# Reordering one graph-network kernel in four places: ScalarE's steps between copies in layer 0, the tail into layer 1, a short tile's list transfers, and the negative sums of layer 2

## The chip, the cores and the metric

The kernel runs on one core of a Trainium2 chip. The metric is the device time of one execution in microseconds (us). Of the kernel before, three runs gave 1071.43 us in the median (1069.46 to 1074.38). Engines are named as in the profile: PE is TensorE (PEld its weight loads), DVE is VectorE, ACT is ScalarE, POOL is GpSimd and SP is SyncE, which here only issues transfers. Every engine works through its own instructions in the order in which the program gave them, and waits on semaphores for what others produce.

## The reference

Four graph layers on 2708 nodes with 128 features, each behind a LayerNorm and a ReLU. `adj` is a dense float32 matrix of 2708 x 2708 (29 MB) with about 0.6% of it, and the diagonal, not zero.

```python
# --- layer 0 ---
h = jnp.maximum(_layernorm(x, axis=-1), 0.0)
x = x + (adj.T @ h) * (1 / adj.sum(axis=0))[:, None]          # 1/0 taken as 0
# --- layer 1 ---
h = jnp.maximum(_layernorm(x, axis=-1), 0.0)
s, d = h @ msg_w[:, :D].T, h @ msg_w[:, D:].T
messages = jax.nn.gelu(s[:, None, :] + d[None, :, :] + msg_b, approximate=False)
aggregated = jnp.einsum('ijd,ij->id', messages, adj)
new = concatenate([h, aggregated], -1) @ upd_w.T + upd_b
x = x + layernorm(gelu(new) + h) * ln_w + ln_b
# --- layer 2 ---
h = jnp.maximum(_layernorm(x, axis=-1), 0.0)
msg = jax.nn.relu((adj @ h) @ W_msg.T + b_msg)
x = x + _gru_cell(msg, h, W_ih, W_hh, b_ih, b_hh)
# --- layer 3: two attention heads, mask = (adj > 0) or the diagonal ---
```

## The kernel before, in words

The nodes are cut into 22 tiles of 128 rows (`NT`; the last has 20, `TAIL`), and these into six groups: five of four tiles, the last of two. Columns are also counted in blocks of 124 (`JB`, 22 of them), because layer 1 works on lists: for every row and block the eight largest entries and their places.

**Layer 0** (0 to about 224 us) reads `adj` once. The loop over `order` goes through five column cuts c (some 512 wide) and for each through six row groups s; a sixth, narrow cut c = `LAST` = 5 (tiles named `z`) is worked beside c = 4. For each (c, s): VectorE lists the rows (`list_cut`, MAX8 and FIND_INDEX8, lines 346 and 348); GpSimd copies the blocks near the diagonal without the diagonal (`mask_near`); `work_cut` has PE transpose the tile (line 387), ScalarE copy the transpose to SBUF (`aT`, line 391), ScalarE's queue write it to `adjT` in memory (line 354, one copy behind), and PE add `adj.T @ h` up in PSUM (`products`, line 373, with a column of ones for the column sums). Cut tiles come from a ring of four buffers, loaded by SP's queue three steps ahead. ScalarE also does LayerNorm steps: `sum_rows` (line 249), `sum_squares` (line 256), whose small steps go to GpSimd, and `normal_rows` (line 136); in c = 0 for the rows of `x`, in a block after each `work_cut`, later for the finished group c - 1, whose new rows are made by `spread` (line 430). `turn_rows`, `destinations` and `split_destinations` prepare `d` of layer 1 for a group. Group 4 and 5 are entered on VectorE by `enter` (reciprocal at line 417, sum into `xs` at 439, statistics) and `rows`. The narrow cut's piece s - 1 is worked after (4, s), its last piece after the loop, and its lists (`list_last`) are taken between layer 1's first steps.

**Layer 1** (to about 600 us) takes one tile per `period(t)`. Before the first, a list of steps written out by hand (`for step, n in (...)`, lines 985 to 996) fills the pipe. In a period, `pass_on` has PE transpose the rows' places (`p_w`, line 740), ScalarE copy them, and SP send them to memory (`passed`, line 744) and back to all partitions (`spread`, line 746); `columns` compares them on VectorE (line 754), which PE's `p_m` products need (lines 805 and 809). `finish_rows` wants `later` (lines 661 and 662, also SP). Tile 21 (20 rows) is listed with other geometry: `load_wide` in period 14, `list_wide` at the end of period 15 (`WIDE_AT`), MAX8 and FIND_INDEX8 on up to 120 partitions (lines 634 and 636) and then twelve small transfers on SP's queue (line 639) that bring the results to `val` and `col`.

**Layer 2** (603 to 785 us) reads `adjT` in six chunks of 512 columns, in five pieces each (`aggregate`; three buffers `a2`): load by SP's queue, three or four ScalarE sums of the negative parts per piece ("looks", line 1241, which end up in `below` and a flag), masks on VectorE and GpSimd, and up to five products into `p_agg` (line 1254). Between products `spend` and `advance` let steps of the chunk before run (`finish_chunk`): `aggc` (line 1265), `hc` (copy at line 151), `p_m` and `msg` (1275, 1277), the gates (1290), `nn` (1298), `h` and `z` (line 136), `z3T` (1331), `hv` (1341 to 1343). Layer 3 follows until 1070 us.

Of the kernel before, what the change touches and what calls it, by code (L numbers as in the profile page):

```python
# [60 lines left out]
def listed_layers(ctx: ExitStack, tc: tile.TileContext, x, adj, w, out, flag):  # L61
# [184 lines left out]
    def sum_rows(t, k):  # L246
        for q in range(t, t + k):
            junk = pool.tile([P, D], F32, name="junk")
            nc.scalar.activation(junk, xs[:, q, :], AF.Copy, accum_out=flat[:, 0, q : q + 1])
        v = flat[:, 0, t : t + k]  # L250
        nc.gpsimd.tensor_scalar(v, v, -1.0 / D, None, ALU.mult)

    def sum_squares(t, k):
# [5 lines left out]
        shift, ve, rstd, tmp = (flat[:, q, t : t + k] for q in range(4))  # L259
        nc.gpsimd.tensor_scalar(ve, ve, 1.0 / D, EPS, ALU.mult, ALU.add)  # L260
        nc.gpsimd.tensor_tensor(rstd, ve, minus_half[:, 0:k], ALU.pow)
        nc.gpsimd.tensor_tensor(tmp, rstd, rstd, ALU.mult)
        nc.gpsimd.tensor_tensor(tmp, tmp, ve, ALU.mult)
        nc.gpsimd.tensor_scalar(tmp, tmp, -0.5, 1.5, ALU.mult, ALU.add)
        nc.gpsimd.tensor_tensor(rstd, rstd, tmp, ALU.mult)
        nc.gpsimd.tensor_tensor(shift, shift, rstd, ALU.mult)

    def normal_rows(dst, t, k):
        scale_rows(
            [dst[:, q, 0:D] for q in range(t, t + k)], tiles_of(xs, t, k),  # L270
            flat[:, 2, t : t + k], flat[:, 0, t : t + k], AF.Relu,
        )
# [83 lines left out]
    def work_cut(c, s):  # L356
# [24 lines left out]
        for js in turns:  # L381
# [13 lines left out]
            ))  # L395
            if c > 0 and todo and gk == 4:
                products(todo.pop(0))
        for n in todo:
# [26 lines left out]
    def spread(g):  # L425
# [5 lines left out]
        nc.gpsimd.tensor_tensor(xs[:, t : t + k, :], xs[:, t : t + k, :], part_x[:, 0:k, :], ALU.add)  # L431
# [28 lines left out]

    order = [(c, s) for c in range(LAST) for s in range(len(GROUPS))]
    mask_near(0, 0)
    for i, (c, s) in enumerate(order):
        g0, gk = GROUPS[s]
        list_cut(c, s, g0)
        if i == 0:
            scale_rows(
                [h0[:, q, 0:D] for q in range(4)], tiles_of(xs, 0, 4), *factors(*state.pop(("m", -1))), AF.Relu
            )
        for n in range(g0 + 1, g0 + gk):  # L470
            list_cut(c, s, n)
        off = 1 if c < LAST - 1 else 0
        if c > 0 and s == off:
# [7 lines left out]
        if i == 0:  # L481
            sum_rows(*GROUPS[1])
        work_cut(c, s)

        if c == 0:
            for stage, g in (
# [1385 lines left out]
```

## Time and profile before

| | |
|---|---|
| median of three runs | 1071.43 us (1069.46 to 1074.38) |
| the profiled execution | 1072.07 us, span 1070.3 us |
| PE, PEld, DVE | 932.0 us (87%), 815.0 (76%), 791.3 (74%) |
| ACT, POOL | 531.7 us (50%), 473.3 (44%) |
| granted TensorE clock, mean | 0.943 of full speed |
| copies of transposes, line 391 | 122, 67.0 us busy, 75.5 us idle before them |
| products of layer 0, line 373 | 880, 121.5 us |
| products of layer 2, line 1254 | 264, 111.2 us, 19.2 us idle before them (13.2 for transfers) |

A row of instructions gives the start and the busy time in us, the engine and the line, the operation, what it writes and reads, the shape and the number; in brackets stands the idle time of the engine just before it and what ended it. Since engines wait in their own order, an idle engine counts only where others wait for it in turn. Shares of the whole span mix layers: in layer 0 from 60 to 190 us the DMA engines are full, in layers 2 and 3 PE is.

### The profile page before, as it was taken

The page shows a single profiled execution, that of the slowest core. Times are in us where ns is not written, and L with a number is a line of the kernel's source. Part 1 is how long each engine was busy: PE and PEld are TensorE (multiplying, and loading weights), DVE is VectorE, ACT ScalarE, POOL GpSimd, SP SyncE. Part 2 cuts the span into 40 slices and gives each one's busy share as a digit, 9 for nine tenths or more (in the row PEclk, how much of TensorE's full clock was granted, in tenths as well). Part 3 has the DMA queues.
Part 4 walks back from the last instruction along what each step waited for, and adds up shares of the span by engine and source line. Part 5 has one row for each costly group of instructions (what it writes and reads, how often), then busy time and mean ns, then how long its engine had stood idle before and what let it go on. Part 6 is the DMA issues. An engine that isn't in the chain of part 4 may idle for free. (4 is left out here: it accounts for less than half of the span.)

```text
span 1070.3 us, 23391 instructions
## 1 busy us (share of the span) xinstructions
PE 932.0 (87%) x8632; PEld 815.0 (76%) x8632; DVE 791.3 (74%) x2740; ACT 531.7 (50%) x1511; POOL 473.3 (44%) x596
## 2 busy tenths in 40 slices
PE   4899898952999999999699759899979999989983
PEld 3799787842899999999699624344468899989982
DVE  7899899468677788979474445555578977997793
ACT  5645554533666667666476366777732200330142
POOL 6222231322987778997576352334310300250042
PEclk9899899975899999999899879999989999999996
DMA  8799899412333333332221435565410000000000
GB/s 287 236 318 373 280 367 365 153 54 81 118 116 104 118 106 121 102 108 91 82 83 56 148 111 172 183 203 203 124 38 20 8 8 1 2 15 6 2 15 16
DMA packets 77091, 133.65 MB, mean 125 GB/s; under 512 B 13980, under 2 KB 29456, under 8 KB 76966
## 3 DMA queue, kind: packets, MB, share of 16 engines
q1 hardware_dynamic: 56986, 99.92, 28.4%
q10 hardware_dynamic: 19980, 32.14, 8.3%
q8 instruction: 70, 1.15, 0.4%
q14 instruction: 55, 0.45, 0.1%
HBM read 85.41 MB, written 30.87 MB: 109 GB/s over the span
## 5 line engine op out<-in xcount | busy, mean ns | idle before, releaser
L723 POOL TENSOR_SCALAR put<-count,line,value 128x128 f32<-128x128 f32 x176 | 202.1, 1161 | 40.3 <-DVE value L712 27.1
L1106 PE MATMUL att<-hv,wt 128*128 128x129 f32 x1672 | 195.5, 278 | 8.8 <-DVE wt L1076 7.3
L1106 PEld LDWEIGHTS att<-hv,wt 128*128 128x128 f32 x1672 | 191.8, 194 | 11.9 <-DVE wt L1076 7.2
L809 PE MATMUL p_m<-d,cols 124*128 124x128 bf16 (+1 forms) x1452 | 164.3, 222 | 7.5 <-DVE cols L754 7.5
L805 PE MATMUL p_m<-s,sel 128*128 128x128 bf16 x1452 | 163.7, 222 | 6.1 <-ACT g L817 6.0
L1076 DVE SCALAR_TENSOR_TENSOR wt<-row,lift,mask 128x1024 f32<-128x1024 f32 (+1 forms) x132 | 138.1, 1075 | 24.5 <-PE att L1106 24.4
L120 POOL TENSOR_TENSOR n_r<-n_r,minus_half 128x4 f32<-128x4 f32 (+1 forms) x27 | 38.9, 1440 | 241.3 <-DVE n_r L119 237.5
L1254 PE MATMUL p_agg<-a,hs 128*128 128x512 f32 (+2 forms) x264 | 111.2, 563 | 19.2 <-DMA a<-adjT 13.2
L830 PE MATMUL agg<-put,g 128*128 128x128 f32 (+1 forms) x968 | 122.9, 279 | 0.0
L373 PE MATMUL sums<-h,a 128*128 128x129 f32 (+1 forms) x880 | 121.5, 287 | 0.0
L830 PEld LDWEIGHTS agg<-put,g 128*128 128x128 f32 x968 | 113.6, 192 | 0.0
L373 PEld LDWEIGHTS sums<-h,a 128*128 128x128 f32 (+1 forms) x880 | 112.6, 202 | 0.9 <-issue 0.2
L805 PEld LDWEIGHTS <-sel 128*128 128x128 bf16 x1452 | 105.1, 99 | 7.8 <-issue 7.3
L809 PEld LDWEIGHTS <-cols 124*128 124x128 bf16 (+1 forms) x1452 | 104.4, 99 | 7.9 <-DVE cols L754 7.9
L391 ACT COPY aT<-p_T 128x512 f32<-128x512 f32 (+2 forms) x122 | 67.0, 564 | 75.5 <-PE p_T L387 47.6
L732 ACT ACTIVATE put<-mine,value 128x128 f32<-128x128 bf16 x308 | 100.5, 391 | 0.0
L817 ACT ACTIVATE g<-p_m 128x512 f32<-128x512 f32 x132 | 72.7, 551 | 55.8 <-PE agg L830 43.1
L1254 PEld LDWEIGHTS p_agg<-a,hs 128*128 128x128 f32 (+1 forms) x264 | 48.3, 196 | 67.8 <-issue 52.0
L387 PE MATMUL p_T<-ident,a 128*128 128x128 f32 (+1 forms) x440 | 72.6, 286 | 30.4 <-ACT aT L391 23.9
L348 DVE FIND_INDEX8 col<-val,a 128x8 uint16<-128x124 f32 x342 | 91.5, 278 | 0.0
L346 DVE MAX8 val<-a 128x8 f32<-128x124 f32 x342 | 78.7, 270 | 12.1 <-DMA a<-in_adj 12.1
L387 PEld LDWEIGHTS p_T<-ident,a 128*128 128x128 f32 (+1 forms) x440 | 53.4, 146 | 39.3 <-ACT aT L391 27.5
(269 smaller groups left out, 1571.8 us busy)
## 6 DMA issues: line engine op xcount, KB each, us to landing
adjT<-aT ACTq DMA_DIRECT2D x105, 256.0 KB
a<-adjT SPq DMA_DIRECT2D x20, 1280.0 KB
spread<-passed SPq DMA_DIRECT2D x22, 704.0 KB
later<-sel SPq DMA_DIRECT2D x22, 616.0 KB
a<-in_adj SPq DMA_DIRECT2D x5, 1152.0 KB
a<-in_adj SPq DMA_DIRECT2D x5, 1120.0 KB
a<-in_adj SPq DMA_DIRECT2D x5, 1088.0 KB
a<-in_adj SPq DMA_DIRECT2D x5, 1056.0 KB
```

The source lines that it names most:

```text
L346: nc.vector.max(val[0:m, n, b, :], v)
L348: nc.vector.max_index(col[0:m, n, b, :], val[0:m, n, b, :], v)
L373: nc.tensor.matmul(accs[c][q // 2][0:k, q % 2, :], a[0:m, n - g0, e : e + k], h0[0:m, n, :], start=(n == 0 and q % 2 == 0), stop=(n == NT ...
L387: nc.tensor.transpose(p[0:k, i * iw + q * P : i * iw + q * P + m], a[0:m, q, e : e + k], ident[0:m, 0:m])
L723: nc.gpsimd.tensor_scalar(st["put", 0][:, b, :], count, st["line"][:, b : b + 1], st["value"][:, b : b + 1], ALU.is_equal, ALU.mult,)
L732: nc.scalar.activation(st["put", 1][:, b - HP, :], st["mine"][:, b - HP, :], AF.Identity, scale=st["value"][:, b : b + 1])
L805: nc.tensor.matmul(p[:, b - b0, :], st["sel"][:, b, :], s3[:, q, t % 2, :], start=(q == 0), stop=False)
L809: nc.tensor.matmul(p[:, b - b0, :], st["cols"][0:kb, b, :], d3[0:kb, b, q, :], start=False, stop=(q == 2))
L830: nc.tensor.matmul(agg, g[:, b - 4 * k, :], put, start=(b == 0), stop=False)
L1076: nc.vector.scalar_tensor_tensor(wt[:, 0:n], row[:, k, c : c + n], lift[:, j, k : k + 1], mask[:, j, c : c + n], op0=ALU.max, op1=ALU.mult,)
L1106: nc.tensor.matmul(banks[s // 3][:, s % 3, :], wt[:, q * P : (q + 1) * P], hv[:, j, k, :], start=(v < 2 and s // 3 not in touched), stop=( ...
L1254: nc.tensor.matmul(pa[:, 0:n], h[0:k, j, :], a[0:k, j - j0, 0:n], start=(j == 0), stop=(j == NT - 1))
```

## The change

Four groups of edits, none of which alters the arithmetic that PE does.

In layer 0 `sum_rows`, `sum_squares`, `normal_rows` and `spread` become generators, and `work_cut` takes one step of them (two in cut 0) after each copy of a transpose, and the rest behind the last. The normal rows of group 0 no longer precede the copies of the first step, they are steps among them; the statistics of group 1 are taken by VectorE's `moments` and `factors`. The narrow cut's pieces are worked after (4,1) to (4,4) by a table `PARTS`, all before (4,5), with `mask_near` for each ahead; `turn_rows(3)` stands before (4,5).

After the loop, the narrow cut's sums are copied at once, group 5 is entered before group 4, and the written-out list of layer 1's first steps is rearranged to fit.

`list_wide` no longer issues its twelve transfers; `place_wide` does so in period 16, at k = 3, behind `columns`.

In layer 2 the looks of a piece stand behind products 2 and 4 of the piece (or at its end) instead of behind its load.

```diff
--- before.py
+++ after.py
@@ -243,33 +243,40 @@
             nc.scalar.copy(dst[1], r)
             nc.gpsimd.tensor_tensor(dst[2], r, dst[1], ALU.subtract)
 
-    def sum_rows(t, k):
+    def sum_rows(g):
+        t, k = GROUPS[g]
         for q in range(t, t + k):
             junk = pool.tile([P, D], F32, name="junk")
             nc.scalar.activation(junk, xs[:, q, :], AF.Copy, accum_out=flat[:, 0, q : q + 1])
-        v = flat[:, 0, t : t + k]
-        nc.gpsimd.tensor_scalar(v, v, -1.0 / D, None, ALU.mult)
-
-    def sum_squares(t, k):
+            if q == t + k - 1:
+                v = flat[:, 0, t : t + k]
+                nc.gpsimd.tensor_scalar(v, v, -1.0 / D, None, ALU.mult)
+            yield
+
+    def sum_squares(g):
+        t, k = GROUPS[g]
         for q in range(t, t + k):
             junk = pool.tile([P, D], F32, name="junk")
             nc.scalar.activation(
                 junk, xs[:, q, :], AF.Square, bias=flat[:, 0, q : q + 1], accum_out=flat[:, 1, q : q + 1]
             )
-        shift, ve, rstd, tmp = (flat[:, q, t : t + k] for q in range(4))
-        nc.gpsimd.tensor_scalar(ve, ve, 1.0 / D, EPS, ALU.mult, ALU.add)
...
-        nc.gpsimd.tensor_tensor(shift, shift, rstd, ALU.mult)
-
-    def normal_rows(dst, t, k):
-        scale_rows(
-            [dst[:, q, 0:D] for q in range(t, t + k)], tiles_of(xs, t, k),
-            flat[:, 2, t : t + k], flat[:, 0, t : t + k], AF.Relu,
-        )
+            if q == t + k - 1:
+                shift, ve, rstd, tmp = (flat[:, r, t : t + k] for r in range(4))
+                nc.gpsimd.tensor_scalar(ve, ve, 1.0 / D, EPS, ALU.mult, ALU.add)
...
+                nc.gpsimd.tensor_tensor(shift, shift, rstd, ALU.mult)
+            yield
+
+    def normal_rows(dst, g, rstd=None, shift=None):
+        t, k = GROUPS[g]
+        for q in range(k):
+            r, b = (flat[:, 2, t : t + k], flat[:, 0, t : t + k]) if rstd is None else (rstd, shift)
+            scale_rows([dst[:, t + q, 0:D]], [xs[:, t + q, :]], r[:, q : q + 1], b[:, q : q + 1], AF.Relu)
+            yield
 
     RING = 4
     WINDOW = CH + 16 * (len(GROUPS) - 2)
@@ -353,7 +360,9 @@
         if written:
             nc.scalar.dma_start(*written.pop())
 
-    def work_cut(c, s):
+    def work_cut(c, s, between=()):
+
+        steps = iter(between)
 
         g0, gk = GROUPS[s]
         t0, tk = GROUPS[c]
@@ -393,8 +402,12 @@
             written.append((
                 adjT[0:k, js[0] : js[0] + n, i0 : i0 + iw], aT[0:k, 0 : n * iw].rearrange("p (j i) -> p j i", j=n)
             ))
+            for _ in range(2 if c == 0 else 1):
+                next(steps, None)
             if c > 0 and todo and gk == 4:
                 products(todo.pop(0))
+        for _ in steps:
+            pass
         for n in todo:
             products(n)
 
@@ -428,7 +441,9 @@
         part_x = pool.tile([P, 4, D], F32, bufs=1, name="part_x")
         for q in range(k):
             nc.scalar.activation(part_x[:, q, :], sums_of(g, q), AF.Identity, scale=inv[:, t + q : t + q + 1])
-        nc.gpsimd.tensor_tensor(xs[:, t : t + k, :], xs[:, t : t + k, :], part_x[:, 0:k, :], ALU.add)
+            if q == k - 1:
+                nc.gpsimd.tensor_tensor(xs[:, t : t + k, :], xs[:, t : t + k, :], part_x[:, 0:k, :], ALU.add)
+            yield
 
     def enter(g):
 
@@ -458,19 +473,53 @@
     for q in range(2):
         nc.gpsimd.memset(wheres[q], 0.0)
 
+    def in_turn(*steps):
+        for step in steps:
+            yield from step
+
+    def first_steps(s):
+
+        if s == 0:
+            return in_turn(
+                sum_rows(2), normal_rows(h0, 0, *state.pop(("f", 0))), normal_rows(h0, 1, *state.pop(("f", 1)))
+            )
+        return in_turn(*(
+            step for ok, step in (
+                (s < LAST, sum_squares(s + 1)), (s < LAST - 1, sum_rows(s + 2)), (s < LAST, normal_rows(h0, s + 1))
+            ) if ok
+        ))
+
+    def next_steps(c, s):
+
+        off = 1 if c < LAST - 1 else 0
+        stage = s - 1 - off
+        if stage == 0:
+            return spread(c - 1)
+        if stage == 1:
+            return sum_rows(c - 1)
+        if stage == 2:
+            return sum_squares(c - 1)
+        if stage == 3:
+            return normal_rows(h, c - 1)
+        return ()
+
+    PARTS = {1: (0,), 2: (1, 2), 3: (3,), 4: (4, 5)}
     order = [(c, s) for c in range(LAST) for s in range(len(GROUPS))]
     mask_near(0, 0)
     for i, (c, s) in enumerate(order):
         g0, gk = GROUPS[s]
         list_cut(c, s, g0)
         if i == 0:
-            scale_rows(
-                [h0[:, q, 0:D] for q in range(4)], tiles_of(xs, 0, 4), *factors(*state.pop(("m", -1))), AF.Relu
-            )
-        for n in range(g0 + 1, g0 + gk):
-            list_cut(c, s, n)
-        off = 1 if c < LAST - 1 else 0
-        if c > 0 and s == off:
+            state["f", 0] = factors(*state.pop(("m", -1)))
+            list_cut(c, s, g0 + 1)
+            state["m", 1] = moments(tiles_of(xs, *GROUPS[1]), "n0")
+            list_cut(c, s, g0 + 2)
+            state["f", 1] = factors(*state.pop(("m", 1)))
+            list_cut(c, s, g0 + 3)
+        else:
+            for n in range(g0 + 1, g0 + gk):
+                list_cut(c, s, n)
+        if c > 0 and s == (1 if c < LAST - 1 else 0):
             invert(c - 1)
         if i + 1 < len(order):
             mask_near(*order[i + 1])
@@ -478,36 +527,19 @@
             load_cut(*order[i - 1 + RING])
         if c == LAST - 2:
             load_cut(LAST, s)
-        if i == 0:
-            sum_rows(*GROUPS[1])
-        work_cut(c, s)
-
-        if c == 0:
-            for stage, g in (
-                ((sum_rows, 2), (sum_squares, 1), (sum_rows, 3), (sum_squares, 2), (normal_rows, 1)),
-                ((sum_rows, 4), (sum_squares, 3), (normal_rows, 2)),
-                ((sum_rows, 5), (sum_squares, 4), (normal_rows, 3)),
-                ((sum_squares, 5), (normal_rows, 4)),
-                ((normal_rows, 5),),
-                (),
-            )[s]:
-                stage(h0, *GROUPS[g]) if stage is normal_rows else stage(*GROUPS[g])
-        elif s == 1 + off:
-            spread(c - 1)
-        elif s == 2 + off:
-            sum_rows(*GROUPS[c - 1])
-        elif s == 3 + off:
-            sum_squares(*GROUPS[c - 1])
-        elif s == 4 + off:
-            normal_rows(h, *GROUPS[c - 1])
+        if (c, s) == (LAST - 1, LAST):
+            turn_rows(LAST - 2)
+        work_cut(c, s, first_steps(s) if c == 0 else next_steps(c, s))
         if c > 1 and s == 0:
             turn_rows(c - 2)
         if c > 1 and s == 1:
             destinations(c - 2)
         if c > 1 and s == 3:
             split_destinations(c - 2)
-        if c == LAST - 1 and s > 0:
-            work_cut(LAST, s - 1)
+        if c == LAST - 1:
+            for z in PARTS.get(s, ()):
+                mask_near(LAST, z)
+                work_cut(LAST, z)
 
         if (c, s) == (0, 3):
             nc.sync.dma_start(msg_wT, w["msg_wT"])
@@ -523,20 +555,19 @@
             nc.gpsimd.tensor_copy(src_self[:, 0, :], msg_wT[:, 0, :])
             nc.gpsimd.tensor_tensor(src_self[:, 1, :], msg_wT[:, 0, :], msg_wT[:, 1, :], ALU.add)
 
-    def list_last(n):
-        list_cut(LAST, n // 4, n)
-
-    for n in range(4):
-        list_last(n)
-    enter(LAST - 1)
-    turn_rows(LAST - 2)
-    destinations(LAST - 2)
-    work_cut(LAST, LAST)
     write_one()
     for q, k in ((0, P), (1, TAIL)):
         nc.scalar.copy(last_sums[0:k, q, :], accs[LAST][0][0:k, q, :])
-    for s in range(len(GROUPS)):
-        mask_near(LAST, s)
+
+    def list_last(n):
+        list_cut(LAST, n // 4, n)
+
+    list_last(0)
+    enter(LAST)
+    for n in range(1, 4):
+        list_last(n)
+    enter(LAST - 1)
+    destinations(LAST - 2)
     l0.close()
 
     gate_b = late.tile([P, 2], F32, name="gate_b")
@@ -634,6 +665,10 @@
                 nc.vector.max(tops[0:m, q, :], cols[0:m, q, :])
             for q, m in enumerate(rows_of):
                 nc.vector.max_index(tops_at[0:m, q, :], tops[0:m, q, :], cols[0:m, q, :])
+            state["tops"] = tops, tops_at
+
+        def place_wide():
+            tops, tops_at = state.pop("tops")
             for i, (b, k) in enumerate(pieces):
                 for dst, src in ((val, tops), (col, tops_at)):
                     nc.sync.dma_start(
@@ -952,6 +987,8 @@
                     put_more(t + 1, k)
                 if k == 3 and c:
                     columns(t + 1)
+                if k == 3 and t == WIDE_AT + 1:
+                    place_wide()
                 if k == 3 and b:
                     place(t + 2)
                 if k == 4 and a:
@@ -984,12 +1021,12 @@
 
         puts = ExitStack()
         for step, n in (
-            (count_rows, 0), (rank, 0), (list_last, 4), (select_rows, 0), (describe, 0), (rows, 4),
-            (list_last, 5), (list_last, 6), (count_next, 0), (turn_rows, 4), (split_destinations, 3),
-            (finish_rows, 0), (fetch_both, 0), (rank, 1), (destinations, 4), (enter, 5), (place, 0), (pass_on, 0),
-            (sources, 0), (select_rows, 1), (split_destinations, 4), (rows, 5), (describe, 1),
-            *((list_last, n) for n in range(7, 12)), (columns, 0), (turn_rows, 5), (destinations, 5),
-            (finish_rows, 1), (fetch_both, 1), (rank, 2), (split_destinations, 5), (place, 1), (select_rows, 2),
+            (count_rows, 0), (rank, 0), (rows, 5), (list_last, 4), (select_rows, 0), (describe, 0), (rows, 4),
+            (turn_rows, 5), (split_destinations, 3), (list_last, 5), (list_last, 6), (count_next, 0), (turn_rows, 4),
+            (finish_rows, 0), (destinations, 4), (fetch_both, 0), (rank, 1), (destinations, 5),
+            (split_destinations, 4), (place, 0), (pass_on, 0), (split_destinations, 5), (sources, 0),
+            (select_rows, 1), (describe, 1), *((list_last, n) for n in range(7, 12)), (columns, 0),
+            (finish_rows, 1), (fetch_both, 1), (rank, 2), (place, 1), (select_rows, 2),
             *((list_last, n) for n in range(12, 17)), (describe, 2), *((list_last, n) for n in range(17, NT)),
             (close_lists, 0),
         ):
@@ -1233,15 +1270,6 @@
             nc.sync.dma_start(a[:, 0:whole, 0:n], adjT[:, j0 : j0 + whole, c : c + n])
             if whole < jn:
                 nc.sync.dma_start(a[0:TAIL, whole, 0:n], adjT[0:TAIL, NT - 1, c : c + n])
-            for m, q0, q1 in ((P, 0, min(2, whole)), (P, 2, min(4, whole)), (P, 4, whole), (TAIL, whole, jn)):
-                if q1 > q0:
-                    junk = pool.tile([P, 2, CH], U8, name="junk2")
-                    i = len(looked)
-                    looked.append(i)
-                    nc.scalar.activation(
-                        junk[0:m, 0 : q1 - q0, 0:n], a[0:m, q0:q1, 0:n], AF.Relu, scale=-1.0,
-                        accum_out=below[0:m, i : i + 1],
-                    )
@@ -1256,6 +1284,18 @@
                 )
                 spend(n / CH)
                 advance()
+                look = {2: ((P, 0, min(2, whole)),), 4: ((P, 2, min(4, whole)),)}.get(j - j0, ())
+                if j == j0 + jn - 1:
+                    look = ((P, 0, whole), (TAIL, whole, jn)) if jn < PIECE else (*look, (P, 4, whole))
+                for m, q0, q1 in look:
+                    if q1 > q0:
+                        junk = pool.tile([P, 2, CH], U8, name="junk2")
+                        i = len(looked)
+                        looked.append(i)
+                        nc.scalar.activation(
+                            junk[0:m, 0 : q1 - q0, 0:n], a[0:m, q0:q1, 0:n], AF.Relu, scale=-1.0,
+                            accum_out=below[0:m, i : i + 1],
+                        )
 
         def finish_chunk(t0, k0, pa):
```

More of the change, by code (lines that the diff above doesn't have):

```diff
@@ L258, in sum_squares @@
             )
-        shift, ve, rstd, tmp = (flat[:, q, t : t + k] for q in range(4))
-        nc.gpsimd.tensor_scalar(ve, ve, 1.0 / D, EPS, ALU.mult, ALU.add)
[L261 to L265, printed above, removed]
-        nc.gpsimd.tensor_tensor(shift, shift, rstd, ALU.mult)
-    def normal_rows(dst, t, k):
-        scale_rows(
-            [dst[:, q, 0:D] for q in range(t, t + k)], tiles_of(xs, t, k),
-            flat[:, 2, t : t + k], flat[:, 0, t : t + k], AF.Relu,
-        )
+            if q == t + k - 1:
+                shift, ve, rstd, tmp = (flat[:, r, t : t + k] for r in range(4))
+                nc.gpsimd.tensor_scalar(ve, ve, 1.0 / D, EPS, ALU.mult, ALU.add)
+                nc.gpsimd.tensor_tensor(rstd, ve, minus_half[:, 0:k], ALU.pow)
+                nc.gpsimd.tensor_tensor(tmp, rstd, rstd, ALU.mult)
+                nc.gpsimd.tensor_tensor(tmp, tmp, ve, ALU.mult)
+                nc.gpsimd.tensor_scalar(tmp, tmp, -0.5, 1.5, ALU.mult, ALU.add)
+                nc.gpsimd.tensor_tensor(rstd, rstd, tmp, ALU.mult)
+                nc.gpsimd.tensor_tensor(shift, shift, rstd, ALU.mult)
[6 more added lines that the diff above has]
+            yield
     RING = 4
```

## The prediction

> **What bounds the kernel now.** I read the page first (busy shares, then the slices), then the busy time in stretches of 20 us, then the order of instructions with the idle time ahead of each in the four places that the change touches. The chain of waits was of no use: it holds the last microseconds alone. Everything is summed against the profiled execution: 1072.07 us, of which the span is 1070.3; the median of the three runs is 1071.43, so 0.64 us comes off at the end.
>
> ```profile
> span 1070.3 us, 23391 instructions
> PE 932.0 (87%) x8632; PEld 815.0 (76%) x8632; DVE 791.3 (74%) x2740; ACT 531.7 (50%) x1511; POOL 473.3 (44%) x596
> ```
>
> PE at 87% is an average over stages with different limits; the stretches show which.
>
> ```profile
> 20.00:40.00 20.00, 15.47 (x120) 14.69 (x120) 20.00 (x136) 18.66 (x74) 9.29 (x30) 0.91 0.58 189
> ...
> 60.00:80.00 20.00, 20.00 (x182) 20.00 (x182) 19.93 (x137) 10.91 (x28) 2.70 (x5) 1.00 1.02 345
> ...
> 160.00:180.00 20.00, 16.57 (x139) 15.44 (x139) 19.14 (x131) 9.35 (x25) 2.24 (x7) 1.00 1.05 379
> ...
> 220.00:240.00 20.00, 9.13 (x63) 6.43 (x61) 14.25 (x51) 7.37 (x23) 6.83 (x16) 0.70 0.14 43
> ...
> 520.00:540.00 20.00, 14.09 (x167) 14.07 (x168) 10.34 (x19) 5.71 (x18) 11.38 (x12) 0.74 0.39 126
> ...
> 700.00:720.00 20.00, 19.45 (x55) 9.38 (x54) 9.78 (x25) 14.74 (x42) 8.34 (x5) 1.00 0.58 199
> ```
>
> Columns after the width: PE, PEld, DVE, ACT and POOL busy, granted clock, DMA share, GB/s. From 20 to 40 us VectorE and ScalarE are full and the DMA engines are not; from 60 to 190 the DMA engines are full; at 220 nothing is (a chain across engines); at 520 PE falls out of an otherwise full stage; in layer 2 PE is the bound.
>
> **Part 1, layer 0.** In column 0 ScalarE's LayerNorm steps stand in one block behind the four copies, and the next transposes wait for it:
>
> ```profile
> 26.33 1.85 PE L387 MATMUL p_T<-ident,a 128*128 128x128 f32 x8 [3.90 <-ACT aT L391]
> ```
>
> After the change two steps stand between two copies, and group 1's sums are taken on VectorE: four sums at .29 and four squares at .39 us leave ScalarE (1.17 + 1.54 = 2.7 us); VectorE gets eight BatchNorm instructions (1.9 us, by 236.13's kind) and the factors (1.27 us, 227.15 to 228.46), 3.2 us in a stretch where it is full. Walking the first four steps with these spacings I get the products' ends 3.7, 4.6, 3.75 and 2.75 us earlier than the 21.55, 32.60, 38.50 and 44.46 of the trace. What reaches the end is less, since the full DMA stretch from 60 on moves up only by DMA time won before it. In 2 us slices the DMA engines idle for 11 us in all before 60 (shares of .33, .61, .03, .24, .31 and so on), but VectorE's lists also hold the tile buffers, and they get longer. I take -3 us, near the 2.75 of the last step walked. Ends: -6 (half of the 11 plus a little, and above every product's gain), and +3 (VectorE's whole 3.2 us passed on, since it is busy 20.00 of 20). The narrow pieces 2 to 4 are now transposed sooner after their loads were issued; a load that is late there costs the same order, and the total of PE work to 224 does not change.
>
> **Part 2, from layer 0 to layer 1.** The last column's tail is reordered. Before, VectorE had group 4 entered early and then waited for PE:
>
> ```profile
> 215.50 0.17 DVE L417 RECIPROCAL inv_deg<-sums 128x2 f32<-128x2 f32 x1 [14.25 <-PE sums L373]
> ...
> 224.27 0.18 DVE L646 CAST ends<-p_r 128x22 bf16<-128x22 f32 x1 [4.26 <-PE p_r L645]
> ...
> 234.70 0.15 DVE L417 RECIPROCAL inv_deg<-sums 128x2 f32<-128x2 f32 x1
> ```
>
> The narrow piece's products now stand ahead of (4,5), but ScalarE's copies of its sums queue behind the hidden-row copy and the two aT copies, so VectorE can enter group 5 at about 221.3 (PE's work to there is the same sum). Then on VectorE in order: enter(5) 2.1 (234.70 to 236.82), lists 1 to 3 2.55 (3 x .85), enter(4) 3.6 (215.50 to about 219.1), the counts .55, a row's rank .4: ends of rank 0 near 230.5 instead of 224.27, and selecting tile 0 ends 7.2 us later. That is won back in part, because enter(5) (2.1) is gone from 234.70, and the waits of 1.01, .59, .47 and 1.48 us between 234 and 247 shrink as ScalarE's and PE's steps have had their time. I take +3.8: 7.2 less 2.1 and less about 1.3 of 3.55 us of waits. Ends: +1.5 (7.2 - 2.1 - 3.55) and +6 (only 1.2 won back). PE has idle time here (9.13 of 20), so what is later on VectorE is later for all.
>
> **Part 3, the short tile's lists.** Twelve small DMAs stand on SP's queue ahead of the transfer that period 16 waits for:
>
> ```profile
> 516.08 0.72 SPq L639 DMA_DIRECT2D col<-tops_at  x1
> 516.90 0.45 SPq L744 DMA_DIRECT2D passed<-where_T  x1
> 519.88 0.35 SPq L746 DMA_DIRECT2D spread<-passed  x1
> ...
> 524.90 0.95 DVE L754 TENSOR_SCALAR cols<-spread,part 128x2816 bf16<-128x2816 bf16 x1 [9.84 <-DMA spread<-passed]
> ...
> 525.91 0.50 PE L809 MATMUL p_m<-d,cols 124*128 124x128 bf16 x3 [6.85 <-DVE cols L754]
> 526.21 0.53 PE L805 MATMUL p_m<-s,sel 128*128 128x128 bf16 x3
> ```
>
> They start at 507.40, .77 us apart, to 516.8; `passed` could have gone at about 504.4. By the starts of p_w, period 16 takes 24.3 us (503.82 to 528.13) where its kind takes 14.5 to 16.0, and period 17 takes 16.9 against 15.2: an excess of 10 to 11.5. In the changed order `passed`, `spread` and both `later` of period 16 go first, and the twelve follow at about 514.9 and end at 524.1. The next `passed` would be wanted near 521.6, so it is 2.5 us late; but between `passed` and the reading of its columns there are 12.1 us in a period without the stall (475.23 to 487.38), of which the transfers need some 6.3 (1.3 to the second issue, 5.0 from 519.88 to 524.90). So 5.8 us of lateness are hidden. The rows of tile 21 are counted in period 17, after the landing. The move itself adds no instruction. I take -9.3: 8.2 to 9.1 of period 16 and about half of period 17's 1.7 us. Ends: -11.5 (all of the excess) and -6 (lateness of 2.5 us and a wait for the counts left).
>
> A rule to weigh: after the wait of 6.85 us above, three matmuls took .53 us instead of the .33 elsewhere, for 4.9 us (525.91 to 530.8), at a granted clock of .74 over the stretch; these cost 1.85 us (4.9 x (1 - .33/.53)). [...]
>
> **Part 4, layer 2.** The sums of negatives ("looks", 72 of them) take ScalarE 1.21 us for 128x1024, .75 for 128x512. Each now stands behind the product it goes with, and so one piece later in ScalarE's order, across the steps that PE waits for:
>
> ```profile
> 672.85 0.61 ACT L1241 ACTIVATE junk<-a 128x512 uint8<-128x512 f32 x1
> ...
> 674.22 0.56 ACT L1265 COPY aggc<-p_agg 128x512 f32<-128x512 f32 x1
> ...
> 675.17 1.05 ACT L1241 ACTIVATE junk<-a 128x1024 uint8<-128x1024 f32 x1
> ...
> 675.31 1.12 PE L1275 MATMUL p_m<-aggc,W_msgT 128*128 128x512 f32 x2 [1.02 <-ACT hc L151]
> ...
> 679.54 0.70 PE L1289 MATMUL p_rz<-msg,W_ihT 128*128 128x512 f32 x1 [0.53 <-ACT msg L1277]
> ...
> 706.60 1.12 PE L1254 MATMUL p_agg<-a,hs 128*128 128x512 f32 x2 [0.55 <-DMA a<-adjT]
> ```
>
> PE already waits for hc here, so what ScalarE does ahead of it is added. In chunks 2 and 4 a look of 1024 comes before z, where ScalarE had 1.25 us idle, and is free; behind z stand 1024, 512, 512, 20x512 instead of 512, 20x512: aggc and hc are 1.21 + .75 = 1.96 us later. The three looks between hc and msg are gone, and with them the wait of .53: +1.4 each. In chunks 3 and 5, 1024, 1024 and 512 (3.2 us) come between z and the rest; PE had about .6 us of other work there (p_hv at 707.57): +2.6 each. Sum 2 x 1.4 + 2 x 2.6 = 8.0. Lower end +3: PE finds the freed slots behind hc useful and the early gates give back the rest (.53 and .6 a chunk are all that the rows show, so this leaves 1.2 a chunk at two chunks and nothing at half of the others). Upper end +11: 2.75 for each of four chunks, when the loads wait too.
>
> **Sum.** -3 + 3.8 - 9.3 + 8.0 = -0.5 us against 1072.07, 1071.57; less .64 this is 1070.9, and I say 1071. The bounds alone make 1058 (-6 + 1.5 - 11.5 + 3) and 1082 (+3 + 6 - 6 + 8).
>
> **Rivals.** Faster, A: layer 0 pays in full. PE's waits for copies in 20 to 60 us (8.2 us) fall and the 11 us of idle DMA time are mostly refilled: -9 instead of -3, so 1065. For it: VectorE and the DMA engines alternate, neither is the bound throughout. Against: VectorE is at 20.00 of 20 and gets 3.2 us more.
>
> Faster, B: layer 2 costs 3 instead of 8, since looks no longer hold ScalarE's queue until a transfer lands: 1066. For it: at the layer's start PE lost 12.61 us to `a`. Against: in the steady chunks ScalarE's order, not the landing, ended the waits.
>
> Slower, C, the loads of layer 2. There are three `a` buffers; a look that comes up to 3.8 us later (a z step of 1.65 and looks of 1.21, .75) releases its buffer that much later, and the next load's issue on SP with it. Landing took 6 to 7.6 us, and at 706.60 PE already waited .55 for one. If the release passes straight on, four chunks cost up to 3.7 each, 14.8 in place of 8.0: 1078. It becomes slower than the half per cent below when layer 2 costs above 13.9, 3.5 us a chunk.
>
> Slower, D: the change of part 3 gives little, because the twelve DMAs now hold the next `passed` instead: with a gain of 3 the time is 1077. Against it are the 5.8 us of slack.
>
> **How the numbers follow.** Half a per cent, 5.4 us, is about what a measurement can tell from no change: 1066.1 to 1076.8. The sum's own case, .42, with 1066 to 1077 as its range. A and B together .28, 1060 to 1066. C .20 and D .10, above 1077. To leave out no more than 2 in 10 the range goes from 1061 to 1081: the lower bounds of parts 1 and 4 are both reached only below it, the upper bounds together only above it. Faster .28, same .42, slower .30.
>
> **What would show it.** Part 1: products of (0,3) end near 41.7, and the DMA share of 1.0 begins a few us earlier. Part 2: the first rank's ends at about 230, less the shift from part 1, and place(1) some 4 us late against layer 0's end. Part 3: no wait above 2 us for `spread` between 505 and 545, a p_w interval of 15 to 16.5 in period 16, clock 1.00. Part 4: PE's wait for hc of 2.5 to 3.5 us in chunks 2 to 5, 28 to 32.7 us between p_m's becoming 30 to 35, more PE waits for `a` if C holds. I am wrong if the sums of two parts change sign: if hc comes earlier because ScalarE was not behind, or if the lists' reordering lets rank 0 start at 224.

## The result, and the profile after

The changed kernel takes 1079.01 us in the median of six runs (1078.55 to 1080.08); the kernel before, now also over six runs, 1070.64 (1066.53 to 1074.38). The ratio is 1.0079, 95% interval 1.0054 to 1.0103: slower, where no change was called the likeliest case. The profiled executions, 1078.55 and 1072.07 us, are 6.5 us apart, and the distance can be followed from mark to mark:

| stretch | before, us | after, us | difference | forecast |
|---|---|---|---|---|
| start to the third p_w (parts 1 and 2) | 284.22 | 285.96 | +1.7 | +0.8 |
| to the first p_m of layer 2 (part 3) | 363.15 | 355.39 | -7.8 | -9.3 |
| to the first att of layer 3 (part 4) | 138.66 | 154.33 | +15.7 | +8.0 |
| to the end | 284.25 | 281.07 | -3.2 | 0 |

So the first three parts together came within 2.4 us of what was said (one by one they did not, see below), and layer 2 lost twice what was said. The head of the changed kernel's page, and four of the stretches that were shown of the kernel before (columns after the width: PE, PEld, DVE, ACT and POOL busy, granted clock, DMA share, GB/s):

```profile
span 1076.8 us, 23389 instructions
PE 937.5 (87%) x8632; PEld 817.0 (76%) x8632; DVE 794.8 (74%) x2754; ACT 529.7 (49%) x1495; POOL 471.7 (44%) x589
```

```profile
20.00:40.00 20.00, 15.71 (x132) 14.53 (x133) 20.00 (x137) 16.22 (x63) 7.37 (x24) 1.00 0.81 253
...
220.00:240.00 20.00, 6.79 (x50) 5.12 (x48) 17.98 (x83) 5.98 (x16) 3.95 (x6) 0.55 0.11 36
...
520.00:540.00 20.00, 20.00 (x276) 19.90 (x276) 13.63 (x20) 11.93 (x37) 16.26 (x14) 0.94 0.23 75
...
700.00:720.00 20.00, 17.76 (x51) 8.79 (x51) 8.37 (x19) 14.30 (x40) 4.74 (x3) 0.91 0.53 189
```

The DMA share from 20 to 40 us rose from .58 to .81, so ScalarE's steps between copies do what they should. From 520 to 540 PE is full instead of 14.09. From 220 to 240 VectorE is busier and PE idler. And from 700 to 720 both PE's share and its granted clock fell, from 19.45 at 1.00 to 17.76 at .91, though PE has the same work. PE's work did not grow, yet its busy time in layer 2's stretch went from 128.9 to 137.3 us, and its idle time from 9.7 to 17.1.

The tail of layer 0, on VectorE:

```profile
219.06 0.17 DVE L430 RECIPROCAL inv_deg<-sums 128x2 f32<-128x2 f32 x1 [23.78 <-ACT sums L560]
...
228.14 0.18 DVE L681 CAST ends<-p_r 128x22 bf16<-128x22 f32 x1 [0.29 <-PE p_r L680]
```

VectorE stands idle for 23.78 us until ScalarE's late copy of the narrow cut's sums, and then has the whole chain to the first ranks ahead of it: 8.4 us from the last products (219.75) to the cast, which in the kernel before followed them (224.11) by .16 us.

SP's queue in period 16 (start, duration, issue):

```profile
506.05 0.30 SPq L779 DMA_DIRECT2D passed<-where_T  x1
507.43 0.36 SPq L781 DMA_DIRECT2D spread<-passed  x1
515.04 0.56 SPq L696 DMA_DIRECT2D later<-sel  x1
515.70 0.84 SPq L697 DMA_DIRECT2D later<-sel  x1
516.59 1.04 SPq L674 DMA_DIRECT2D val<-tops  x1
...
525.67 0.72 SPq L674 DMA_DIRECT2D col<-tops_at  x1
526.49 0.45 SPq L779 DMA_DIRECT2D passed<-where_T  x1
```

`passed` is issued before the twelve, and VectorE's wait of 9.84 us for `spread` is gone. Period 16 takes 17.9 us between p_w starts (505.51 to 523.41) instead of 24.3. The twelve start at 516.59, 1.7 us later than forecast, so the next `passed` stands right behind them.

PE in layer 2, at the first product of three chunks, and at the next `p_hv` and p_m:

```profile
669.67 2.07 PE L1282 MATMUL p_agg<-a,hs 128*128 128x512 f32 x2 [2.91 <-DMA a<-adjT]
...
703.66 2.08 PE L1282 MATMUL p_agg<-a,hs 128*128 128x512 f32 x2 [2.12 <-DMA a<-adjT]
...
736.74 1.27 PE L1282 MATMUL p_agg<-a,hs 128*128 128x512 f32 x2 [3.02 <-DMA a<-adjT]
...
770.96 0.70 PE L1379 MATMUL p_hv<-w_x,z3T 128*128 128x260 f32 x2 [1.86 <-ACT z3T L1371]
773.27 1.22 PE L1315 MATMUL p_m<-aggc,W_msgT 128*128 128x512 f32 x1 [1.60 <-ACT hc L151]
```

Three times, where one chunk's products follow another's, PE now waits for `a`, where it had waited .55 us at most, and no longer for hc; the fourth time it waits for z3T and hc. Two matmul records, one product, take 1.02 us at full clock; after the first two waits they take 2.07.

What held the loads back stands among the waits of SP's queue (what it waited for: us in total, times, longest), before and after:

```profile
SPq L1233 <- ACT junk L1241: 18.0, 8, 8.0
SPq L1270 <- ACT junk L1295: 65.5, 24, 8.3
```

The issue of a load waits for a look (`junk`) to let go of the buffer, 24 times instead of 8. The load that PE waits for at 669.67 is issued 22.55 us behind the first p_m (663.90), 18.96 us behind it in the kernel before (666.33).

### The profile page after: what moved, and what is told of

It is laid out like the page before. It is cut to its first block, busy times and chain, and to the rows that moved or that the text cites. A ratio compares the mean times of both kernels' runs of the same rounds, so it can differ in the third digit from the quotient of the medians.

```text
span 1076.8 us, 23389 instructions
## 1 busy us (share of the span) xinstructions
PE 937.5 (87%) x8632; PEld 817.0 (76%) x8632; DVE 794.8 (74%) x2754; ACT 529.7 (49%) x1495; POOL 471.7 (44%) x589
## 5 line engine op out<-in xcount | busy, mean ns | idle before, releaser
L758 POOL TENSOR_SCALAR put<-count,line,value 128x128 f32<-128x128 f32 x176 | 199.5, 1147 | 31.6 <-DVE value L747 31.4
L1113 DVE SCALAR_TENSOR_TENSOR wt<-row,lift,mask 128x1024 f32<-128x1024 f32 (+1 forms) x132 | 138.7, 1082 | 21.9 <-PE att L1143 21.8
L1282 PE MATMUL p_agg<-a,hs 128*128 128x512 f32 (+2 forms) x264 | 115.1, 580 | 28.2 <-ACT junk L1295 12.1
L396 PE MATMUL p_T<-ident,a 128*128 128x128 f32 (+1 forms) x440 | 74.4, 290 | 27.1 <-ACT aT L400 20.5
```

Of the source, the lines that this page charges most:

```text
L396: nc.tensor.transpose(p[0:k, i * iw + q * P : i * iw + q * P + m], a[0:m, q, e : e + k], ident[0:m, 0:m])
L758: nc.gpsimd.tensor_scalar(st["put", 0][:, b, :], count, st["line"][:, b : b + 1], st["value"][:, b : b + 1], ALU.is_equal, ALU.mult,)
L1113: nc.vector.scalar_tensor_tensor(wt[:, 0:n], row[:, k, c : c + n], lift[:, j, k : k + 1], mask[:, j, c : c + n], op0=ALU.max, op1=ALU.mult,)
L1282: nc.tensor.matmul(pa[:, 0:n], h[0:k, j, :], a[0:k, j - j0, 0:n], start=(j == 0), stop=(j == NT - 1))
```

## The experiments

Which part of the change loses the time was asked first, then by which mechanism, and last whether parts 1 and 2 are worth what the trace seems to say.

**Looks back, all else as changed**

```diff
+            for m, q0, q1 in ((P, 0, min(2, whole)), (P, 2, min(4, whole)), (P, 4, whole), (TAIL, whole, jn)):
+                ...                       # the look, behind the piece's load
-                look = {2: ((P, 0, min(2, whole)),), 4: ((P, 2, min(4, whole)),)}.get(j - j0, ())
...
```

> The changed kernel with the looks of layer 2 back behind each piece's load (all else as changed). From the first p_m of layer 2 to the first att of layer 3 the kernel before took 138.7 us (647.37 to 786.03), the changed one 154.3 (641.35 to 795.68). Theory L (the looks' place is the whole loss of layer 2): 138 to 140 us there, PE waits for a of 0.6 us or less behind the first chunk, clock 1.00 from 650 to 790, and the whole near 1066 (1079.0 less 15.7, plus the 2.7 that layer 3 gave back). Rival S (layer 2 is slower because it starts at another moment or with other things in flight): 148 us or more there, 1074 or more in all.

Measured 1065.34 us (ratio to before .9916, .9884 to .9947), 138.64 us from first p_m to first att, the largest wait for `a` .84 us, and no half clock between the first p_m (646.53) and 784. The looks' place is the whole loss of layer 2. Parts 1 to 3 together are a gain.

**Only the looks moved**

```diff
 # kernel before
-            for m, q0, q1 in ((P, 0, min(2, whole)), ...):     # looks behind the load
+                look = {2: ((P, 0, min(2, whole)),), 4: ((P, 2, min(4, whole)),)}.get(j - j0, ())
...
```

> The kernel before with nothing but the looks of layer 2 moved behind the products. Theory L: first p_m to first att 152 to 156 us instead of 138.7, half-clock stretches in it, the whole near 1084 (1070.6 plus 13). Rival S: 141 us or less, 1074 or less.

Measured 1086.91 us (1.0117, 1.008 to 1.0155), 157.23 us in the stretch. The loss comes with the looks alone, and is a little larger here: PE is idle for 18.2 us instead of 17.1, and at half clock for 23.9 us instead of 20.5.

**The looks late, but reading other data**

```diff
-                            junk[0:m, 0 : q1 - q0, 0:n], a[0:m, q0:q1, 0:n], AF.Relu, scale=-1.0,
+                            junk.rearrange("p q c -> p (q c)")[0:m, 0 : (q1 - q0) * n],
+                            h.rearrange("p t d -> p (t d)")[0:m, 0 : (q1 - q0) * n], AF.Relu, scale=-1.0,
```

> The changed kernel with each look at its new place and of the same size, but reading the layer's rows h instead of the piece a (so the negative entries of adj are not looked for); a look then no longer holds an a buffer. Theory R (the loss is the late release of the buffers: the load starts late, PE waits 2 to 3 us for a, and the clock is halved for a window after each wait): waits for a behind the first chunk 0.6 us or less, no half-clock stretch from 650 to 790, first p_m to first att 139 to 147 us (what is left is ScalarE's order ahead of hc), the whole 1066 to 1072. Rival Q (ScalarE's order delays aggc and hc): hc is as late as in the changed kernel, 151 us or more, 1076 to 1080 in all.

Measured 1071.88 us (1070.14 to 1082.70; 1.0006, .9979 to 1.0033): inside what was written for the late buffers. But the whole misleads: the stretch still takes 151.85 us, the rival's number, and what made the whole short is that the first p_m came at 635.52 instead of 641.35, since no look holds the buffers when layer 2 starts either: the load of the first chunk's fourth piece is issued at 618.32 instead of 624.35, and PE goes on at 624.63 instead of 630.57. The waits for `a` are gone (SP's queue waits for no look, and the load that was issued 22.55 us behind the first p_m is issued 18.70 behind it), and in their place stands the wait that the forecast had named:

```profile
659.76 0.59 PE L1282 MATMUL p_agg<-a,hs 20*128 20x512 f32 x1
660.28 0.66 PE L149 MATMUL p_h<-ident,hs 128*128 128x128 f32 x4
660.77 1.02 PE L1282 MATMUL p_agg<-a,hs 128*128 128x512 f32 x2
661.63 0.60 PE L149 MATMUL p_z<-ident,z 128*128 128x128 f32 x4
665.19 1.13 PE L1316 MATMUL p_m<-aggc,W_msgT 128*128 128x512 f32 x2 [2.96 <-ACT hc L151]
```

The same wait of some 3 us comes at a third chunk (3.09 at 733.33), and waits of 1.5 to 1.9 for z3T and 1.6 for hc twice. So a late look does two things that stop PE for about as long: it stands in ScalarE's order ahead of z3T and hc, and it holds the buffer that the next load needs. Taking the buffers' hold away uncovers the order; the reverse, an early hc with the buffers still held, was not run, but the landing of the load does not depend on hc.

**Useless products in the waits**

```diff
+            if jn < PIECE and 0 < t0 < 16:
+                warm = accs.tile([P, CH], F32, tag=f"acc{(t0 // 4 + 1) % 2}", name="p_warm")
+                for q in range(4):
+                    nc.tensor.matmul(warm, ident, h.rearrange("p t d -> p (t d)")[:, 0:CH], start=True, stop=True)
             for j in range(j0, j0 + jn):
```

> The changed kernel with four products of no use (identity by rows of h, 128x512, about 1.9 us, into a free PSUM bank) on PE ahead of the products of the narrow last piece of chunks 1, 2 and 3, where PE waits 2.9, 2.1 and 3.0 us for a. The loads come no earlier. Theory C (each wait of some 2 us or more is followed by a stretch of 3.4 us at half clock, and these stretches are about half of layer 2's loss): the stretches at 669, 703 and 738 us go, first p_m to first att about 149 us instead of 154.3, the whole near 1074. Rival W (the waits alone cost; the slower products come from something else in flight): 154 us or more there and 1079 or more in all.

The four products took 3.6 us, not 1.9 (a float32 product of this size takes two records of some .45 us, and I had counted one; likewise the 264 of line 1254 in the table of the kernel before are records, two for each of 132 products), so they cover the waits whole. Measured: 149.78 us in the stretch and 1075.24 us in all (1.0032, 1.0007 to 1.0057), 3.8 below the changed kernel, with more work on PE (the intervals of the two ratios, to 1.0057 and from 1.0054, just meet). The half-clock stretches at 669, 703 and 738 us are gone. The same stretches of time in the changed kernel,

```profile
664.00:669.00 5.00, 2.76 (x9) 0.90 (x7) 2.47 (x10) 4.88 (x11) 2.73 (x2) 1.00 0.77 261
669.00:673.00 4.00, 3.33 (x8) 1.92 (x9) 1.23 (x1) 2.30 (x7) 2.52 (x1) 0.57 0.85 274
```

and with the products filled in:

```profile
664.00:669.00 5.00, 5.00 (x13) 2.05 (x12) 2.64 (x10) 4.84 (x12) 2.90 (x2) 1.00 0.76 254
669.00:673.00 4.00, 4.00 (x16) 2.03 (x15) 1.23 (x1) 3.31 (x8) 2.52 (x1) 1.00 0.82 262
```

The clock (the column ahead of the DMA share) stays at 1.00 where it had been .57. This shows that the slower products were the clock's, and that in these three places the clock followed the waits.

**Only the transfers of the short tile**

```diff
+                if k == 3 and t == WIDE_AT + 1:
+                    place_wide()
                 if k == 3 and b:
                     place(t + 2)
```

> The kernel before with nothing but the twelve transfers of the short tile moved behind the later transfers of period 16. If the move gains by itself what the changed kernel's trace shows: period 16 takes 15 to 18 us between p_w starts instead of 24.3, and the whole is 7 to 8 us shorter than before, near 1063. Rival (the next passed waits behind the twelve and gives the gain back): 1068 or more, with a wait for spread of over 3 us in period 17.

Measured 1062.75 us (.9902, .9864 to .9941), and in a second timing, further down, 1061.16 (.9905, .9886 to .9924). Period 16 takes 16.2 us (505.44 to 521.63). The move is worth some 10 us by itself.

**Looks behind msg**

```diff
+            if jn < PIECE or (j0 == 0 and t0 > 0):
+                kept.append(looks)
+            else:
+                looks()
...
             nc.scalar.activation(half_n[:, 0:n], ph[:, 0:n], AF.Identity, bias=half_b, scale=0.5)
+            while kept:
+                kept.pop(0)()
```

> The kernel before with the transfers moved (part 3), and in layer 2 only the looks of each chunk's narrow last piece and of the next chunk's first piece moved, behind half_n: nothing is then between the last products and aggc, hc and msg, and the looks run while PE does the seven products of the gates. If ScalarE's order ahead of hc is what PE waits for, the waits of 1.0, .8 and .5 us for hc and msg go and the whole is 2 to 4 us below 1062.75; if the two later releases of a buffers make loads late instead, waits for a of 1 to 3 us appear and it is 1063 to 1070.

Measured 1066.78 us (.9942, .9923 to .9962), against 1062.75 for the same kernel without this edit; 144.67 us in the stretch, against 138.52. The waits for hc and msg are gone as expected, and only one wait for `a` above .3 us (.80) is there; but neither forecast saw the wait that came:

```profile
678.70 0.72 ACT L1314 ACTIVATE nn<-nn,b_ih 128x512 f32<-128x512 f32 x1 [0.97 <-DVE nn L1313]
679.42 1.28 ACT L1357 ACT_TABLE_LOAD   x1
680.72 0.17 ACT L1357 ACTIVATE hv<-p_hv 128x2 f32<-128x2 f32 x1
```

```profile
681.80 0.68 PE L1355 MATMUL p_hv<-w_x,z3T 128*128 128x260 f32 x2 [2.69 <-DVE hv L1361]
```

The looks delay the gates and nn, the exponentials of hv stand behind nn and a table load of 1.28 us, and PE waits for the bank that hv reads. This place in ScalarE's order was not free for 4 us of looks, though ScalarE is idle a quarter of the time (in the kernel before it is busy for 101.77 of the 138.66 us from the first p_m to the first att).

**Parts 1 and 2 alone**

```diff
 # changed kernel
-                if k == 3 and t == WIDE_AT + 1:
-                    place_wide()
...                                       # and the looks behind the load
```

> The changed kernel with the looks and the twelve transfers back at their old places: parts 1 and 2 alone. In the changed kernel and in two variants that have the same program up to 280 us, the third p_w starts 1.7, 7.4 and 2.1 us later than in the kernel before (284.22), so this should be 1.5 to 7 us slower than before. If the sum of parts 1 and 2 were the forecast's -3 + 3.8, it would be within 1.5 us of before.

Measured 1073.37 us (1.0012, 1.0000 to 1.0025) and +2.8 at the third p_w: 1.3 us by the ratio, within the forecast's 1.5 and just short of the 1.5 to 7 that the traces had suggested.

**Part 1 with part 3, and part 2 with part 3**

```diff
 # the first: the narrow cut, the tail and the list of first steps as in the kernel before
-    PARTS = {1: (0,), 2: (1, 2), 3: (3,), 4: (4, 5)}
...
 # the second: no `between` in work_cut, and the steps in blocks as in the kernel before
-        work_cut(c, s, first_steps(s) if c == 0 else next_steps(c, s))
+        work_cut(c, s)
...
```

> Of the change, ScalarE's steps between copies (part 1) and the moved transfers (part 3), with the narrow cut, the tail and the first steps of layer 1 as before. Against the moved transfers alone (1062.75): if part 1 gains what the forecast took, 3 us, 1060, and the first cast of ends near 221; if VectorE's 3.2 us more in a stretch where it is full is passed on, 1066 and the cast at 227; if part 1 is worth nothing beyond 60 us, since the DMA engines set the time from there, 1063 and 224 to 225.

> Of the change, the narrow cut's pieces before (4,5), the tail and the rearranged first steps (part 2) and the moved transfers (part 3), with ScalarE's steps in blocks as before. Against 1062.75 for the moved transfers alone: if the tail costs what the forecast took, 1066 to 1067, the first cast of ends 6 us later than 224.3, and the second p_w 3 to 4 us later; if the entering of group 5 ahead of group 4 costs nothing, 1062 to 1063.

The first took 1060.89 us (.9903, .9885 to .9920), the second 1068.11 (.9957, .9934 to .9980). Against 1062.75 that looks like -1.9 for part 1 and +5.4 for part 2. The first cast of ends comes at 222.25 in the first and at 234.97 in the second, 10.7 us later than 224.3 and not 6; the second p_w of the second kernel comes 7.3 us later than with part 3 alone (266.03 against 258.74), not 3 to 4. Since the end of layer 0 moves by up to 5.7 us between executions of the same program (219.75, 225.40, 220.41, 220.75 and 220.31 in five with parts 1 and 2), part 1 was timed again beside part 3 alone, with more runs:

> Parts 1 and 3 once more, beside part 3 alone on the same chip, since layer 0 of one and the same program ended up to 5.7 us apart from run to run. If part 1 gains 2 to 3 us as the first pair of traces says (third p_w at 282.19 against 285.23): about 1060 and 2 to 3 us below part 3 alone. If that was the spread of layer 0: within 1 us of it.

> Part 3 alone, beside parts 1 and 3: about 1063, 2 to 3 us above the other if part 1 gains, within 1 us of it if not.

1061.56 and 1061.16 us, ratios .9902 and .9905. Part 1 gains nothing that can be measured. In the traces the products of column 0 end 5.4 and 3.0 us sooner with part 1 (55.54 against 60.98, 56.60 against 59.56), and of that 3.0 and .5 us are left at the last products of layer 0.

**The sums' copies early**

```diff
             for z in PARTS.get(s, ()):
                 mask_near(LAST, z)
                 work_cut(LAST, z)
+            if s == LAST - 1:
+                for q, k in ((0, P), (1, TAIL)):
+                    nc.scalar.copy(last_sums[0:k, q, :], accs[LAST][0][0:k, q, :])
...
     write_one()
-    for q, k in ((0, P), (1, TAIL)):
-        nc.scalar.copy(last_sums[0:k, q, :], accs[LAST][0][0:k, q, :])
```

> The changed kernel with the looks at their old place and ScalarE's copies of the narrow cut's sums moved ahead of (4,5), so that VectorE can enter group 5 and take the first lists while PE still works at (4,5). If the late tail comes from these copies: the first cast of ends about 4 us sooner after the last products of layer 0 (4 to 5 us instead of 8.4), and the whole 2 to 4 us below the 1065.3 of the same kernel with the copies late. If VectorE's entering of group 4 and PE set it, 1065 still.

From the last products to the cast of ends it is 5.3 us instead of 8.4, and to the third p_w 63.1 instead of 66.2. The whole is 1064.37 us against 1065.34, which their spreads (1060.57 to 1065.15 and 1062.74 to 1069.57) do not tell apart. So the late copies make 3.1 of the 8.2 us by which the cast came later (8.4 us behind the last products instead of .16); where the other 5.1 come from was not tried, and that the copies are worth 2 to 4 us of the whole is not shown.

Of all versions the one with parts 1 and 3 (1060.89 and 1061.56) and the one with part 3 alone (1062.75 and 1061.16) are fastest, some 10 us below the kernel before that was timed beside them (1072.7, 1071.46 and 1073.01), and 16 to 18 below the changed one.

## Why the prediction was wrong

The predicted 1071 had the measured 1079 in its range, but on the sign it was wrong: no change was the likeliest case, and the kernel is slower by .8%. (Its 1082 was added up with 8 for part 4, where its own upper end was 11; with that the bounds end at 1085.) By its steps:

**Part 4, the term of 8.0 us, failed.** It was worked out as ScalarE's delay of hc, handed on to PE as idle time. Idle time it got nearly right, 7.3 us more (17.06 against 9.73), but by luck: the longer waits are mostly for `a` and not for hc. What it left out is the granted clock behind the waits. In the changed kernel stretches of half clock of 3.4 us begin at 669.3, 703.5, 737.6, 771.7 (6.8 us long) and 788.8, each within 1 us of the end of a wait of 1.9 to 3.0 us. They make 20.5 us of half clock in the stretch against 1.8 before, and PE's busy time is 8.4 us longer for the same products. The two terms, 7.3 and 8.4, are the 15.7. The products filled into three of these waits took their stretches away and 4.6 us with them (154.33 to 149.78). (There are 84 looks, three to a piece and two to the narrow one, not 72; no term rests on that.)

**Rival C had the right place and the wrong reason for its price.** The waits that the trace shows are for `a`, as it said, 10 us in all from 660 on, and the load is issued 3.6 us later (22.55 against 18.96), near its 3.8. Rival B, with 3 us, is refuted. But the waits for `a` do not add to those for hc: with the buffers freed, hc made PE wait instead (2.96, 1.60, 3.09, 1.60 us). Its 14.8 us is near the 15.7 because it took the wait as long as the delay in four chunks, not because it saw the clock. The chance given to it, .20, was too low: the forecast argued that ScalarE's order, not the landing, ends the waits in the kernel before, and that is no evidence for a kernel in which the looks hold the buffers longer.

**Chunk by chunk.** From p_m to p_m, chunks 2 to 5 take 3.10, 1.65, 2.64 and 3.13 us longer than before (31.04 to 34.61 us now), 10.5 in all, where the forecast had 1.4, 2.6, 1.4 and 2.6. The sixth, narrow chunk was put at nothing, and takes 5.15 us more (25.12 against 19.97): a wait of 1.95 us for `a` stands in it, and 11.5 us of half clock instead of 4.5. These five make the 15.7. So the intervals of 30 to 35 us that the forecast named as its sign came out, with another wait and with the clock in them.

**The slower clock at a wait**, which part 3 had met (a wait of 6.85 us, and a granted clock of .74 from 520 to 540 us), should have been weighed in part 4. Shorter waits came with it too: 1.95, 2.12 and 2.91 us were enough here, and the stretches of half clock last 3.4 us, once 6.8. But longer ones were not enough elsewhere: with the looks on other data, waits of 2.96 and 3.09 us (to 665.19 and 733.33) were followed by no half clock, nor was one of 3.43 us in layer 0 of the kernel before (to 174.93, at a clock of 1.00 in it and behind it), nor were waits of 1.44 and 1.88 us with the products filled in; with the looks behind msg a wait of .80 us was.

In the traces of both kernels the half-clock stretches begin whole multiples of some 3.41 us apart; those of layer 2 in the changed kernel, at 669.32, 703.45, 737.59, 771.72 and 788.79, are 34.13, 34.14, 34.13 and 17.07 us apart. If the time from the first p_m to the first att is cut into slices of this length at these points, the two traces have six slices in which PE idles for 1.91 us or more, all in the changed kernel, and half clock follows each of them; it follows the three with 1.55 to 1.77 us as well, and none with 1.12 us or less. The wait of 3.43 us in layer 0 lies across two slices, with 1.77 and 1.66 us of idle time, and there none followed. What brings the half clock on is not shown by this, and no run tested it.

**Part 3**: -9.3 forecast. The trace of the changed kernel has -7.8 up to layer 2; part 3 alone has -9.8 and -9.1 there in its two traces, and -10 in the whole. Right in mechanism; the twelve began 1.7 us later than worked out, and the next `passed` waits for them, as its slack of 5.8 us allowed. Rival D is refuted.

**Part 2**: +3.8 forecast, bounds 1.5 to 6. The third p_w comes 60.1 us behind the last products of layer 0 in all seven traces with the old tail, and 65.9 to 66.3 us behind them in six with the new one (early copies: 63.1): 6 us, at the upper bound. With part 3 it costs 5.4 us of the whole; in the changed kernel part of it is hidden by products that end earlier. So parts 1 and 2 do not simply add up: together they cost 1.3 us. With part 2, layer 0 ended at 219.75 to 220.75 in four of five traces with part 1, and at 226.57 in the one without; whether part 1 pays there is left open by the spread. VectorE began the tail at 219.06, 2.2 us before the 221.3 of the forecast, and the first cast came at 228.14.

**Part 1**: -3 forecast; less than 1 us could be measured beside part 3, though the products of (0,3) ended 3.8 us sooner (40.70 against 44.46), where 2.75 was worked out. The gain is there and does not last; that the full DMA stretch takes it, as the forecast said, fits, and no run shows it. Rival A is refuted.

**Not foreseen and left open**: from the first att to the end the changed kernel is 3.2 us shorter. The kernel with only the looks moved has it too (281.4 against 284.3 us), but with the looks back it is 282.6, and part 3 alone, traced twice, has 284.0 and 281.9; so no cause is shown.

## What to carry to other kernels

A wait on TensorE may not be over when the data arrives: in layer 2 of the changed kernel each wait of 1.9 us or more was followed by 3.4 us at half clock (one by 6.8), and PE's busy time for the same products was 8.4 us longer. It need not be so (waits of 2.96 and 3.09 us in another run were followed by none), so read the granted clock behind each wait before you price it. Where an engine's order is moved, follow each moved instruction in two directions, to what stands behind it on its engine and to what it holds (a buffer, a bank), because the two waits run side by side, and taking one away may leave nearly the whole: with the buffers free, ScalarE's order still cost 13.2 of the 15.7 us. And when a whole agrees with a theory, look at the stretch that the theory speaks of before believing it.

## What the runs showed of the hardware that I had not expected

- Short waits can cost clock: waits of 1.9 to 3.0 us on TensorE in layer 2 of the changed kernel, in a stage otherwise full, were followed by 3.4 us at half clock (once 6.8), beginning within 1 us of the wait's end. The first four of the stretches began 34.13 us apart. With the looks on other data, waits of 2.96 and 3.09 us were not followed by one.
- More work made the kernel faster: four products of no use in each of three waits took PE's busy time in layer 2's stretch from 137.3 to 139.8 us, the stretch from 154.3 to 149.8 and the whole from 1079.0 to 1075.2.
- A program's first 225 us vary: with the same instructions the last product of layer 0 ended between 219.75 and 225.40 us, so that a gain of 3 us there can be read from no single trace.
